# Local attention on one core: whole cells instead of halves, and TensorE's order by kinds of products

## The chip, the core and the metric

The kernel runs on one core of a Trainium2 chip. A core has TensorE (matrix products from SBUF into PSUM; weights are loaded by its own instruction, PEld in the profile), VectorE (DVE), ScalarE (ACT), GpSimd (POOL) and a queue SP that issues DMA transfers. Each engine runs its own instructions in program order and waits for others through semaphores. PSUM has eight banks, and a bank takes 512 float32 values in each of 128 partitions. The metric is the device time of one execution in microseconds; lower is better.

## The reference, cut to what matters

Two transformer layers run over x of shape (4, 512, 128). The first (16 heads of 8, then a mixture of experts) and the attention of the second take the first 0.7 ms and are not touched. The second layer's feed-forward part is itself a stack of six local-attention layers, and this is where the change is:

```python
for i in range(DEPTH):      # 6
    x = attn_layer(shift_tokens(x), Wqkv[i], q_scale[i], k_scale[i], Wo[i]) + x
    x = ffn_layer(shift_tokens(x), ln_g[i], ln_b[i], W1[i], b1[i], W2[i], b2[i]) + x
```

`attn_layer` projects to q, k and v for 16 heads of 64, normalises q and k to length one, multiplies by scales, rotates (xpos), and attends in windows of 32 tokens: each window of 32 queries sees its own window and the one before, so scores are 32 x 64, with a mask, a softmax and a product with 64 rows of v. `ffn_layer` is a layer norm, two products of width 341 with a gelu gate, and a product back. `shift_tokens` moves half of the features by one token.

## The kernel before

**Cells.** The work of the six layers is cut into 96 cells `(l, b, j)`: layer, batch row, and a group of four heads. A loop over n runs a software pipeline: in the turn of cell n, TensorE takes scores and weighing of cell n (or n-1), norms, scaling and values of cells n+1 and n+2, and the projection of cell nx = n+3. All of it is issued inside a manual schedule: the order written in the loop is the order on each engine, and the scheduler only adds the waits.

**Steps of one cell**, with the names of the code:

- `project(n, w)` (line 831): q (w = 0) or k (w = 1) of four heads, 128 x 1024 float32 into `pq`, which fills two banks and has one buffer. `rotate(n, w)` (841 to 844) makes two VectorE products from `pq` and two GpSimd sums. `square(n, w)` (849) is ScalarE's square of `pq` into `sq`, the last reader of `pq`.
- `norms(n)` (859 to 878): sums of squares on TensorE (`nb`, a 128*32 shape), a maximum on VectorE, logarithm and exponential on ScalarE (each with a table load), and four DMAs that spread the result as `rb`. `scale(n)` (886) multiplies k and q by it on GpSimd; `gather(n, w)` (899) rearranges them by four DMAs each into `kd` and `qd`.
- `values(n)` (910 to 920): v into two `pv2` banks, two ScalarE copies to `vo`, three DMAs that make the shifted copy `ve`.
- `scores(n, u)` (933 to 955): for half u of the windows, two mask products (128*128 shape, bfloat16) and 32 small float32 products (64*32 shape, two records each in the profile) into `s2`; then a maximum and a difference on VectorE into `p`. `exponential` (959) is on ScalarE, `normalise` (964 to 966) is a sum, a reciprocal and a product on VectorE.
- `turn(n, u)` (973, 975): four transposes of p on TensorE (128*128) into the one bank of `ps_t`, and a ScalarE copy to `pT`. `weigh(n, u)` (988, 1000): 32 small products with v (64*64 shape) into `ps_o` and `ps_t`, and two ScalarE copies to `oT`.
- `output(n)` (1008, 1009): after every second cell, eight records of the output projection into `py`, and VectorE adds it to the residual `zT`.

**Feed-forward.** After the fourth cell of a batch row a generator `feed(l, b)` is started. It advances where the loop calls `place(name)` with the name it last yielded: Z (issue the shifted load `xsf` from `zT`), B (mean product `lm`, then `l_xc`), D (square), N, L, X (variance product, logarithm, exponential), A (`xn`, two VectorE operations on `l_xc`), then B and D twice (two hidden products `phf` each, and gelu on ScalarE), C (a gate on VectorE), A (two more hidden products and gates), B (`pyf`, three products, and the sum into `zT`). So one batch row's feed-forward is spread over the next batch row's four cells.

**PSUM.** `nb`, `pv2`, `py2`, `lm`, `lv`, `phf` and `pyf` share a pool of two banks (tag `g`), handed out in program order: each new one waits for the readers of the one two places earlier. `pq` has two banks, `s2` two, `ps_t` and `ps_o` one each.

**The loop's order before** for TensorE is: scores half 0, weighing half 1 of the cell before, norms, projection of q, (output), scores half 1, values, transposes half 0, projection of k, weighing half 0, B's products, transposes half 1.

Of the kernel before, what the change touches and what calls it, by code (L numbers as in the profile page):

```python
# [17 lines left out]
F32 = mybir.dt.float32  # L18
BF16 = mybir.dt.bfloat16
AF = mybir.ActivationFunctionType  # L20
ALU = mybir.AluOpType
# [3 lines left out]
B, S, D = 4, 512, 128  # L25
# [21 lines left out]
def adaln_kernel(ctx: ExitStack, tc: tile.TileContext, a: dict):  # L47
# [368 lines left out]
    class First:  # L416
# [41 lines left out]
        def settle(self):  # L458
            pass
# [307 lines left out]
    with ExitStack() as ph:  # L767
# [77 lines left out]

        def square(n, w):
            d = live[n]
            d["sq", w] = work.tile([P, 2, S], F32, name="sq")
            act(d["sq", w], d.pop("pq"), AF.Square)  # L849

        def norms(n):

            d = live[n]
            nb = bank("nb", (P, S // 2))
            for h in range(2):
                for w in range(2):
                    for x in range(2):
                        c = 32 * (2 * w + x)
                        mm(  # L859
                            nb[c : c + 32, :],  # L860
                            nsel,
                            d["sq", w][:, h, x * (S // 2) : (x + 1) * (S // 2)],
                            start=(h == 0),
                            stop=(h == 1),
                            skip_group_check=True,
                        )
            rn = att.tile([P, S // 2], F32, name="rn")
            vec.tensor_scalar(rn, nb, 1e-24, None, ALU.max)
            place("N")
            act(rn, rn, AF.Ln, scale=65536.0)  # L870
            place("L")
            act(rn, rn, AF.Exp, scale=-0.5, bias=nsh_t)
            place("X")
            rb = d["rb"] = work.tile([P, 2, S], F32, name="rb", bufs=1)
            for w in range(2):
                for x in range(2):
                    c = 32 * (2 * w + x)
                    nc.sync.dma_start(
                        rb[:, w, x * (S // 2) : (x + 1) * (S // 2)],
                        rn[c : c + 32, :].unsqueeze(1).broadcast_to([32, 4, S // 2]),  # L880
                    )
# [6 lines left out]
        def gather(n, w):  # L888

            d = live[n]  # L890
            t = d["k" if w else "q"]
            if w:
                d["k"] = kts[n % 2]
                y = d["k"][:, :, WIN:]
            else:
                y = d["q"] = cel.tile([P, 2, S], F32, name="qd", bufs=2)
            for c in range(2):
                for h in range(2):
                    nc.sync.dma_start(y[h::2, c, :], t[64 * c : 64 * c + 64, h, :])  # L899
# [20 lines left out]
            nc.sync.dma_start(ve[64:96, 1:], vo[96:P, 0 : TB - 1])  # L920


        def scores(n, u):
            d = live[n]
            q, k = d["q"], d["k"]


            if u == 0:
                d["s"] = ps_s.tile([P, 2, UW, GK], F32, name="s2")
            s = d["s"][:, :, 4 * u : 4 * u + 4, :]  # L930
            for w in range(2):
                m = wmask_b[:, 1 if u == 0 and w == 1 else 0, 0:4, :]
                mm(s[:, w], ident_b, m, start=True, stop=False, skip_group_check=True)
            for i in range(4):
                for w in range(2):
                    t0 = (u * UW + 2 * i + (w + i + 1) % 2) * WIN
                    for x in range(4):
                        r, c = slice(64 * (x % 2), 64 * (x % 2) + 64), 32 * ((x + w) % 4)
                        mm(  # L939
                            s[c : c + 32, w, i, :],  # L940
                            q[r, x // 2, t0 : t0 + WIN],
                            k[r, x // 2, t0 : t0 + GK],
                            start=False,
                            stop=True,
                            skip_group_check=True,
                        )
            nm = att.tile([P, 2, 4], F32, name="nm2")
            vec.reduce_max(nm, s, axis=AX.X)  # L948
            p = d["p", u] = att.tile([P, UW, GK], F32, name="p2")
            vec.tensor_tensor(  # L950
                p.rearrange("p (i w) k -> p w i k", w=2),
                s,
                nm.unsqueeze(3).broadcast_to([P, 2, 4, GK]),
                ALU.subtract,
            )

        def exponential(n, u):
            p = live[n]["p", u]
            act(p, p, AF.Exp)  # L959

        def normalise(n, u):
            p = live[n]["p", u]
            sm = att.tile([P, UW], F32, name="sm2")
            vec.reduce_sum(sm, p, axis=AX.X)  # L964
            vec.reciprocal(sm, sm)
            vec.tensor_tensor(p, p, sm.unsqueeze(2).broadcast_to([P, UW, GK]), ALU.mult)  # L966

        def turn(n, u):

            p = live[n].pop(("p", u))  # L970
            pt = ps_t.tile([P, 4, P], F32, name="pt2", tag="pt2")
            for i in range(4):
                tr(pt[:, i, :], p[:, 2 * i : 2 * i + 2, :].rearrange("p w k -> p (w k)"), ident)  # L973
            pT = live[n]["pT", u] = att.tile([P, 4, P], F32, name="pT2")
            nc.scalar.copy(pT, pt)  # L975

        def weigh(n, u):
            d = live[n]
            pT = d.pop(("pT", u))

            po = [ps_o.tile([P, 2, 4, WIN], F32, name="po2"), ps_t.tile([P, 2, 4, WIN], F32, name="po2b", tag="pt2")]
            for i in range(4):
                for x in range(4):
                    c = 64 * (x % 2)
                    for w in range(2):
                        r = slice(64 * w, 64 * w + 64)
                        c1 = 32 * ((x + w) % 4)
                        mm(  # L988
                            po[w][c : c + 64, x // 2, i, :],
                            d["v"][(w + i) % 2][r, 2 * u + i // 2, 64 * x : 64 * x + 64],  # L990
                            pT[r, i, c1 : c1 + 32],
                            start=True,
                            stop=True,
                        )
            if u == 0:
                d["o"] = cel.tile([P, 2, 2, S // 2], F32, name="oT2", bufs=2)
            o = d["o"][:, u].rearrange("p h (a w q) -> p (h a) w q", w=4, q=WIN)
            for w in range(2):
                y = po[w].rearrange("p h (a b) q -> p (h a) b q", b=2)
                nc.scalar.copy(o[:, :, 0::3, :] if w else o[:, :, 1:3, :], y)  # L1000

        def output(n):
# [11 lines left out]
        def feed(l, b):  # L1014
# [38 lines left out]
            yield "B"  # L1053
            ge = [one.tile([P, S], F32, name=f"ge{c}") for c in range(3)]
            t0, t1 = hidden(1, 0), hidden(1, 1)
            yield "D"
            gelu(0, t0)
            gelu(1, t1)
            yield "B"
            t0, t1 = hidden(1, 2), hidden(0, 2)  # L1060
            yield "D"
            gelu(2, t0)
            yield "C"
            gate(2, t1)
# [29 lines left out]
        for n in range(-4, NC + 1):  # L1094
            nx = n + 3 if 0 <= n + 3 < NC else None
            here = 0 <= n < NC
            if here:
                scores(n, 0)
            if 0 <= n + 1 < NC:
                scale(n + 1)  # L1100
                gather(n + 1, 1)
            if n > 0:
                weigh(n - 1, 1)
            if here:
                exponential(n, 0)
            if 0 <= n + 2 < NC:
                norms(n + 2)
            elif n + 2 >= NC:
                for name in "NLX":
                    place(name)  # L1110
            place("C")
            if 0 <= n + 1 < NC:
                gather(n + 1, 0)
            if nx is not None:
                l, b, j = cells[nx]
                if l + 1 < DEPTH:
# [3 lines left out]
                        load_rotations(l + 1)  # L1120
                project(nx, 0)
            if here:
                normalise(n, 0)
            if nx is not None:
                rotate(nx, 0)
            if n > 0 and cells[n - 1][2] % 2 == 1:
                output(n - 1)
            place("Z")
            if n + 4 < NC and cells[n + 4][2] == 0:
                b = cells[n + 4][1]  # L1130
                shifted[b] = shift_in(b, xss[b % 2])
            if here:
                scores(n, 1)
            if nx is not None:
                square(nx, 0)
            if 0 <= n + 2 < NC:
                values(n + 2)
            if here:
                exponential(n, 1)
            place("A")  # L1140
            if here:
                turn(n, 0)
                normalise(n, 1)
            if nx is not None:
                project(nx, 1)
                rotate(nx, 1)
            if here:
                weigh(n, 0)
            place("B")
            if here:  # L1150
                turn(n, 1)
            if nx is not None:
                square(nx, 1)
                l, b, j = cells[nx]
                for b1, j1, w, h in turns:
                    if (b1, j1) == (b, j) and l + 1 < DEPTH:
                        rotations(l + 1, w, h)
            place("D")
        while feeds or running:
            for name in "NLXCZABD":  # L1160
                place(name)


# [102 lines left out]
```

## Time and profile before

| | us |
|---|---|
| three runs, median (lowest to highest) | 2494.04 (2487.45 to 2505.30) |
| the profiled execution, its own time | 2490.49 |
| its span, first to last instruction | 2488.7 |
| busy: TensorE / VectorE / ScalarE / GpSimd | 2182.5 / 1524.1 / 1399.9 / 1072.2 |
| mean granted TensorE clock | 0.944 of full speed |

The time of the profiled execution and its span differ by 1.8 us, which lies around the program's own instructions. In the lines of the profile, "L831" is line 831 of the kernel. A row of the order in time gives start, length, engine, line, operation, out<-in, shape and count; matmul lengths are modelled and overlap the next ones, so the price of a block is read from its start to the next block's start. A float32 product of 128x512 shows as two records. Stretches ("2248.59:2265.77") give busy time and count for each engine, then the granted clock, the share of the DMA engines and GB/s. A wait is "who waited <- for whom: total us, times, longest us".

### The profile page before, as it was taken

How to read it: one execution, taken by the hardware profiler on the slowest of the kernel's cores; microseconds unless marked ns; L12 is line 12 of the kernel's file. 1: busy time of each engine (PE TensorE's matmuls, PEld its weight loads, DVE VectorE, ACT ScalarE, POOL GpSimd, SP SyncE). 2: the span in 40 equal slices, each digit the busy share in tenths (PEclk: the TensorE clock that was granted, in tenths of full speed). 3: DMA queues.
4: the chain of work that ended last, by engine and by line, in shares of the span. 5: the costliest groups of instructions: out<-in, count | busy, mean ns of one | idle time of the engine just before them, and what ended most of it. 6: DMA issues, size and time to landing. Idle time of an engine off the chain costs nothing.

```text
span 2488.7 us, 76520 instructions
## 1 busy us (share of the span) xinstructions
PE 2182.5 (88%) x33628; PEld 1246.4 (50%) x33628; DVE 1524.1 (61%) x2258; ACT 1399.9 (56%) x2211; POOL 1072.2 (43%) x690
## 2 busy tenths in 40 slices
PE   6889999886688888999999888999889899889996
PEld 3345454443245555555555555555555555555553
DVE  3454545333266666777677766767667767677763
ACT  1333344534256566766566665667666666676763
POOL 1000101010365565556555565555665556555550
PEclk8999999888789999999999998999999999999998
DMA  2100000000156645566554844557545565555551
GB/s 73 64 2 1 3 1 1 1 1 1 55 133 157 149 114 127 124 174 148 116 131 113 210 111 112 129 124 191 123 117 125 149 170 120 122 119 135 125 137 27
DMA packets 164760, 251.23 MB, mean 101 GB/s; under 512 B 28742, under 2 KB 90380, under 8 KB 163404
## 3 DMA queue, kind: packets, MB, share of 16 engines
q1 hardware_dynamic: 164428, 246.34, 40.9%
q8 instruction: 264, 4.33, 0.7%
q14 instruction: 68, 0.56, 0.1%
HBM read 34.27 MB, written 1.05 MB: 14 GB/s over the span
## 4 chain that ended last, share of the span: by engine, by line
PE 59%; ACT 13%; DVE 9%; issue 7%; SPq 5%; DMA 4%; POOL 3%; ACTq 0%; DVEq 0%; POOLq 0%
PE pq L831 10%; PE phf L1021 5%; PE s L286 5%; PE py L1008 4%; PE po L988 4%; PE nb L859 3%; ACT sq L849 3%; PE s L939 3%; PE pyf L1072 3%; PE ye L360 3%; PE pv L910 2%; DMA xsf<-zT 2%; PE pt L973 2%; DVE qr L841 2%; SPq L899 2%
## 5 line engine op out<-in xcount | busy, mean ns | idle before, releaser
L831 PE MATMUL pq<-xs,wqkv 128*128 128x512 f32 x768 | 393.8, 637 | 21.6 <-ACT sq L849 20.0
L843 POOL TENSOR_TENSOR kr<-kr,ur 128x512 f32<-128x512 f32 x96 | 122.0, 1271 | 499.4 <-DVE ur L842 460.8
L849 ACT ACTIVATE sq<-pq 128x1024 f32<-128x1024 f32 x192 | 197.1, 1027 | 129.9 <-DVE ur L842 126.1
L975 ACT COPY pT<-pt 128x512 f32<-128x512 f32 x192 | 112.5, 586 | 246.4 <-PE pt L973 246.4
L886 POOL TENSOR_TENSOR qr<-qr,rb 128x1024 f32<-128x1024 f32 x96 | 235.4, 2452 | 0.0
L842 DVE TENSOR_TENSOR ur<-pq,tabs 128x1024 f32<-128x1024 f32 x192 | 232.6, 1212 | 0.0
L843 POOL TENSOR_TENSOR qr<-qr,ur 128x512 f32<-128x512 f32 x96 | 123.4, 1286 | 253.3 <-DVE ur L842 252.0
L831 PEld LDWEIGHTS pq<-xs,wqkv 128*128 128x128 f32 x768 | 141.1, 202 | 180.5 <-issue 149.0
L886 POOL TENSOR_TENSOR kr<-kr,rb 128x1024 f32<-128x1024 f32 x96 | 228.6, 2382 | 6.2 <-DMA rb<-rn 6.2
L404 ACT ACTIVATE p<-s 128x1024 f32<-128x1024 f32 (+3 forms) x160 | 104.0, 701 | 188.9 <-PE s L286 150.5
L173 POOL TENSOR_TENSOR ln_rs<-ln_rs,mhalf 128x4 f32<-128x4 f32 x16 | 16.8, 1050 | 443.9 <-DVE ln_rs L172 443.9
L948 DVE TENSOR_REDUCE nm<-s 128x8 f32<-128x512 f32 x192 | 132.1, 688 | 122.0 <-PE s L939 121.9
L964 DVE TENSOR_REDUCE sm<-p 128x8 f32<-128x512 f32 x192 | 130.5, 680 | 112.5 <-ACT p L959 112.3
L910 PE MATMUL pv<-wqkv,xs 128*128 128x256 f32 x768 | 191.5, 392 | 0.8 <-DVE zT L1009 0.8
L1021 PE MATMUL phf<-l_xc,w 128*128 128x512 f32 (+1 forms) x288 | 154.1, 662 | 42.3 <-ACT vo L917 38.3
L939 PE MATMUL s<-kd,qd 64*32 64x64 f32 x12288 | 172.9, 227 | 19.4 <-DMA qd<-qr 17.5
L966 DVE TENSOR_TENSOR p<-p,sm 128x512 f32<-128x512 f32 x192 | 179.6, 936 | 6.6
L1000 ACT COPY oT<-po 128x256 f32<-128x256 f32 x192 | 71.2, 371 | 197.6 <-PE po2b L988 194.5
L1008 PE MATMUL py<-oT,wo 128*128 128x512 f32 x384 | 172.8, 593 | 0.6 <-ACT ge L1026 0.6
L859 PE MATMUL nb<-sq,nsel 128*32 128x256 f32 x1536 | 117.7, 416 | 62.1 <-ACT ge L1026 51.0
L988 PEld LDWEIGHTS po<-pT,vo 64*64 64x64 f32 x3072 | 126.6, 137 | 89.6 <-ACT pT L975 63.0
L988 PE MATMUL po<-pT,vo 64*64 64x32 f32 x3072 | 164.2, 224 | 7.6 <-ACT pT L975 6.8
(198 smaller groups left out, 4987.2 us busy)
## 6 DMA issues: line engine op xcount, KB each, us to landing
rb<-rn SPq DMA_DIRECT2D x384, 128.0 KB
kd<-kr SPq DMA_DIRECT2D x384, 128.0 KB
qd<-qr SPq DMA_DIRECT2D x384, 128.0 KB
ve<-vo SPq DMA_DIRECT2D x96, 256.0 KB
tabs<-in_rope_dram SPq DMA_DIRECT2D x12, 1024.0 KB
ve<-vo SPq DMA_DIRECT2D x96, 128.0 KB
wqkv<-in_Wqkv_dram SPq DMA_DIRECT2D x6, 1536.0 KB
ve<-vo SPq DMA_DIRECT2D x96, 96.0 KB
```

The source lines that it names most:

```text
L831: mm(pq[:, h, :], layers[l][0][:, c0 : c0 + P], shifted[b], start=True, stop=True)
L842: vec.tensor_tensor(u, d["pq"], t[:, 2 * w + 1], ALU.mult)
L843: pool_e.tensor_tensor(r[:, 0, :], r[:, 0, :], u[:, 1, :], ALU.subtract)
L849: act(d["sq", w], d.pop("pq"), AF.Square)
L859: mm(nb[c : c + 32, :], nsel, d["sq", w][:, h, x * (S // 2) : (x + 1) * (S // 2)], start=(h == 0), stop=(h == 1), skip_group_check=True,)
L886: pool_e.tensor_tensor(t, t, d["rb"][:, w, :].unsqueeze(1).broadcast_to([P, 2, S]), ALU.mult)
L910: mm(pv[:, t, :], shifted[b][:, (y + t) * P : (y + t + 1) * P], layers[l][0][:, c0 : c0 + 4 * HDW], start=True, stop=True,)
L939: mm(s[c : c + 32, w, i, :], q[r, x // 2, t0 : t0 + WIN], k[r, x // 2, t0 : t0 + GK], start=False, stop=True, skip_group_check=True,)
L966: vec.tensor_tensor(p, p, sm.unsqueeze(2).broadcast_to([P, UW, GK]), ALU.mult)
L988: mm(po[w][c : c + 64, x // 2, i, :], d["v"][(w + i) % 2][r, 2 * u + i // 2, 64 * x : 64 * x + 64], pT[r, i, c1 : c1 + 32], start=True, st ...
L1008: mm(py, layers[l][1][:, 2 * j - 2 + y, :], o[:, :, y % 2, :], start=(y == 0), stop=(y == 3))
L1021: mm(t[0:m], w1[:, w * DI + r0 : w * DI + r0 + m], xn, start=True, stop=True)
```

## The change

The halves go away. `scores` makes all windows of a cell in one block (two mask products of twice the width, 64 small products); its two VectorE operations become `settle`, for the whole cell (128x1024); `exponential` and `normalise` work on the whole cell; `turn` makes eight transposes into two banks (`ps_o`, `ps_t`) with two copies; `weigh` makes 64 small products into the same two banks, with two copies of 128x512 each in place of four of 128x256. `norms` is split into `norms` and `invert`, which are called one after the other. `sq` gets three buffers for two, `qd` one for two, `p` and `pT` one. In `feed`, gelu waits at a new place G, which the loop calls right behind B.

The loop's order becomes: projection of q, scores (64*32), weighing of the cell before (64*64), norms (128*32), projection of k, output, values, transposes, B's products. Gather of q moves ahead of the norms' DMAs, and loads of a layer's weights and tables to the head of the turn.

```diff
-                y = d["q"] = cel.tile([P, 2, S], F32, name="qd", bufs=2)
+                y = d["q"] = cel.tile([P, 2, S], F32, name="qd", bufs=1)
...
+        def settle(n):
+            d = live[n]
+            s = d.pop("s")
+            nm = att.tile([P, 2, UW], F32, name="nm2")
             vec.reduce_max(nm, s, axis=AX.X)
-            p = d["p", u] = att.tile([P, UW, GK], F32, name="p2")
+            p = d["p"] = att.tile([P, 2 * UW, GK], F32, name="p2", bufs=1)
...
+            for u in range(2):
+                pt = (ps_o, ps_t)[u].tile([P, 4, P], F32, name="pt2", tag="pt2")
+                for i in range(4):
+                    g = 4 * u + i
+                    tr(pt[:, i, :], p[:, 2 * g : 2 * g + 2, :].rearrange("p w k -> p (w k)"), ident)
+                nc.scalar.copy(pT[:, 4 * u : 4 * u + 4], pt)
...
+            po = [(ps_o, ps_t)[w].tile([P, 2, 2, 4, WIN], F32, name=f"po{w}", tag="pt2") for w in range(2)]
```

The loop body of the turn of cell n, after the change, without the conditions on n and nx:

```python
load_layer / load_rotations            # at two cells of a layer
project(nx, 0)
scores(n)
scale(n + 1); gather(n + 1, 1); gather(n + 1, 0)
rotate(nx, 0); square(nx, 0)
settle(n)
weigh(n - 1)
exponential(n)
norms(n + 2); invert(n + 2)            # places N, L, X inside
place("C")
normalise(n)
project(nx, 1); rotate(nx, 1)
output(n - 1)                          # every second cell
place("Z"); shift_in(...)              # at j = 0
values(n + 2)
square(nx, 1)
place("A")
turn(n)
place("B"); place("G")
rotations(l + 1, w, h)                 # at four cells of a layer
place("D")
```

## The prediction

> **What bounds it now.** I read the page first (shares of the engines, chain that ended last), then the busy times of four consecutive cells, the order of TensorE's instructions in one of them, who waited for whom, and the granted clock behind a long wait.
>
> ```profile
> PE 2182.5 (88%) x33628; PEld 1246.4 (50%) x33628; DVE 1524.1 (61%) x2258; ACT 1399.9 (56%) x2211; POOL 1072.2 (43%) x690
> PE 59%; ACT 13%; DVE 9%; issue 7%; SPq 5%; DMA 4%; POOL 3%; ACTq 0%; DVEq 0%; POOLq 0%
> ```
> TensorE is nearly full, and the chain runs mostly through it. The 96 cells stand at 695 to 2438 us, 18.3 us each; only they change. A quiet group (layer 5, batch 1, cells j = 0 to 3):
>
> ```profile
> 2248.59:2265.77 17.18, 16.13 (x312) 9.80 (x310) 13.05 (x18) 10.03 (x16) 8.55 (x6) 1.00 0.59 132
> 2265.77:2281.72 15.95, 14.67 (x309) 9.07 (x307) 14.27 (x18) 11.43 (x19) 9.64 (x6) 1.00 0.61 148
> 2281.72:2300.24 18.52, 16.95 (x314) 10.04 (x312) 12.11 (x17) 13.89 (x20) 9.82 (x7) 1.00 0.47 102
> 2300.24:2320.26 20.02, 16.41 (x313) 9.72 (x311) 13.08 (x19) 13.16 (x19) 11.02 (x8) 1.00 0.49 122
> ```
> Columns: stretch, its length, busy PE, PEld, DVE, ACT, POOL, clock. At full clock four cells take 71.67 us, of which TensorE works 64.16 and waits 7.5. VectorE works 52.5: 73%, a close second, and that matters below.
>
> ```profile
> 2286.52 1.98 PE L831 MATMUL pq<-xs,wqkv 128*128 128x512 f32 x4
> 2288.34 3.60 PE L1008 MATMUL py<-oT,wo 128*128 128x512 f32 x8
> 2291.78 0.38 PE L933 MATMUL s<-wmask_b,ident_b 128*128 128x256 bf16 x2
> 2292.09 0.86 PE L939 MATMUL s<-kd,qd 64*32 64x64 f32 x64
> 2292.88 1.99 PE L910 MATMUL pv<-wqkv,xs 128*128 128x256 f32 x8
> 2294.71 0.60 PE L973 MATMUL pt<-ident,p 128*128 128x128 f32 x4
> 2295.14 1.88 PE L831 MATMUL pq<-xs,wqkv 128*128 128x512 f32 x4
> ```
> Start to start is a block's price: projection 1.82, output 3.44, masks 0.31, half the scores 0.79, values 1.83, half the transposes 0.43; from the same view half the weighing 1.07 and the norm sums 1.00.
>
> ```profile
> ACT sq L849 <- DVE ur L842: 83.6, 86, 3.5
> PE nb L859 <- ACT ge L1026: 51.0, 39, 1.6
> PE phf L1021 <- ACT vo L917: 38.3, 22, 2.9
> PE lm L1036 <- DMA xsf<-zT: 33.7, 22, 3.6
> ```
> These are the waits that interrupt TensorE (total, times, longest). The first says that the square, last reader of the projection's PSUM, starts only after both rotation products of VectorE.
>
> **What is removed.** Starts of single matmuls in the trace give the price of a change of shape: masks follow each other at 109 ns, the first 64*32 score follows the last mask at 203 (94 more); 64*32 to 64*64 and back to 128*128 costs about 134 over the stride, 64*64 to 128*32 133, 128*32 to 128*128 148, 128*128 to 64*64 93. A cell pays eight such changes before and four after; the four that go are 94+134+93+133 = 0.45 us. The first 128*128 product behind a change also takes 1.82 for 1.72; two of these go, 0.2. Together 0.66 us a cell, 63 us in 96 cells.
>
> ScalarE and VectorE save a fixed part per merged instruction. 128x1024 against 128x512 (rotation product 1.21, zT sum 0.68; square 1.03, copy 0.59) puts 512 more elements at 0.53 and 0.44. So maximum and difference cost 1.22 each for 2x0.69, the exponential 1.07 for 2x0.63, the copy of weighed values 0.59 for 2x0.37: 0.9 us a cell of both engines, none of it on TensorE. The norm wait for gelu (51 us) goes: its bank is now asked for 5.7 us into the next cell, behind projection, scores and weighing. Splitting norms moves nothing; three sq and one qd buffers cost nothing while scores (done at 3.7 us) read qd before the next gather. Gather q now stands ahead of rb in SP's queue, both still 8 us early. The loads of weights and tables stand ahead of a cell's gathers: 0 to 15 us over five layers, I take 5.
>
> **What is added.** The halves gave TensorE work while the other half was in softmax. Now one chain runs per cell, and VectorE holds it in program order: rotate(0), settle, normalise, rotate(1), then output's sum or the feed-forward's scaling. I place one cell, from its first projection (0.00 us), at full clock.
> TensorE: projection 1.72, masks 0.53 with the change, scores 1.44 (to 3.69), weighing 2.00 (5.69), norms 1.00 (6.69), projection 1.82 (8.51), [output 3.43], values 1.73, transposes 0.87: 11.11 without output.
> VectorE: rotate 1.81 to 4.16 (starts 1.14 apart), settle to 6.54. ScalarE: two copies from 5.80, exponential 6.78 to 7.84. VectorE: normalise (1.22+0.21+1.22) 7.90 to 10.60, rotate(1) to 12.87. Where gelu ran in the cell before (j = 2, 3), a table load of 1.28 comes before the exponential: rotate(1) ends at 14.15.
>
> - j=0: output ends 11.94, but its zT sum waits for rotate(1): 13.5. The second values product needs py's bank: 0.8 idle. SP is through with rb at 14.05 (3.6 from the exponential's end through both table loads, then 4x0.64); xsf's issue to lm took 2.96 (2261.41 to 2264.37): lm at 17.0, 1.7 idle; it and the next xs: 18.1.
> - j=1: xn follows rotate(1) (0.68+1.38): 14.8. TensorE is through at 11.97: 2.9 idle; two hidden products: 16.65.
> - j=2: zT sum 14.76; the second values product waits for it from 12.8: 2.05 idle; then 0.86, 0.87, 1.72: 18.3.
> - j=3: values copies stand behind exponential and both table loads, at 12.6: hidden products wait from 10.24 to 13.3, 3.06 idle; then 1.72, 0.87, 2.58: 18.45.
>
> Sum 71.5. Check from the other side: work 4x11.11 + 2x3.43 + 11x0.86 = 60.8, idle 0.8+1.7+0.3+2.9+2.05+3.06 = 10.8: 71.6. Against 71.67 the whole saving is eaten: **0 us at full clock**. Queued behind the values product that waits for zT's sum are the transposes, and behind those the feed-forward and the next cell's projection; behind a waiting phf the same, with VectorE's next rotation waiting in turn: nothing on TensorE fills these holes. The pq loop itself (square ends 13.98 to 18) does not bind.
>
> **The clock.** Three waits of 2 to 3 us a group come in place of pieces below 2, and this trace shows what follows:
>
> ```profile
> 935.20:938.40 3.20, 0.03 (x4) 0.01 (x1) 1.90 (x2) 0.65 (x2) 1.22 (x1) 0.94 0.85 199
> 938.40:941.40 3.00, 2.97 (x8) 1.67 (x8) 0.69 (x1) 0.04 (x1) 3.00 (x3) 0.50 0.63 174
> ```
> After 3.2 us without work the clock is 0.50 for 3.4 us. From 694 to 1300 us I count 7 waits over 2 us (8.3 groups), 5 with such a stretch behind them. Three a group instead of 0.8, times 5/7: 1.5 more stretches, each losing 1.7 us of work that the next step waits for: 2.5 us a group, **60 us** in 24 groups. The Trainium skill speaks against the change here: "TensorE: Matmul & The Clock Gate" (Part 1) has the clock halved after an idle window of about 3.4 us; it names the threshold longer than the waits placed here, so by it alone the 60 us would be 0 and the time 2495. The rows show stretches behind shorter waits too (908.3 to 910.6 idle, then 0.50), so I take the count.
>
> **The sum.** 0 + 60 + 5 = +65 us on the profiled execution's 2490.5 (span 2488.7): 2555. That execution lies 3.5 below the median 2494 of the three runs, which differ by 18, so about 1% is what a measurement can tell; I put 2557 against the median.
>
> **Rivals.**
> - Faster: TensorE stays the bound. If VectorE's order costs no more idle than now (7.5 a group), the saved 63 us come through, and no clock is lost: about 2430. For it: PE 88%. Against: VectorE's 12.9 us to the end of rotate(1) in each cell, with nothing for TensorE left behind the transposes. It decides once idle falls below 9 a group.
> - No change: full-clock balance, stretches at half clock no more frequent than now, because waits of 2 to 3 us straddle a window: 2495, 2470 to 2518.
> - Much slower: the normalising product meets GpSimd on every cell. Its mean is 0.93 against 0.69 alone, 1.51 in one cell here; doubled, it would cost up to 1.2 us more a cell on that VectorE chain, 29 us, and with all four waits a group halving the clock (3.4 stretches more, 24x3.4x1.7 = 139): 2490+29+139 = 2660. For it: GpSimd's scaling lies right ahead; against: it should be through at 7 us.
> - The change does not do what it says: the extra 94 to 148 ns are weight loads rather than the change of shape, and stay. Then 63 us come on top of the forecast: 2620. Against: the excess stands at every change of shape and nowhere else within a block.
>
> **How the numbers follow.** Forecast 0.45; much slower 0.10 and price stays 0.08, both slower; no change 0.17; faster 0.20. The forecast's own range is 2520 to 2600; the range 2455 to 2645 leaves out the outer part of the faster case and of the slower ones. Slower by over 1%: 0.63, within 1%: 0.17, faster: 0.20.
>
> **What would show it.** PE busy time should fall by some 60 us at equal clock. Right: waits phf <- vo of 3 us each, phf <- xn of l_xc near 3 us, values <- zT of 2 us; norms <- gelu gone; more half-clock stretches; j = 1 longer than 15.95, j = 3 shorter than 20.02. Wrong, if idle a group stays near 7.5, if rotate(1) ends before 12 us of a cell, or if the projection waits for the square.

## The result: 9% slower, and the profile after

The changed kernel takes 2715.23 us (median of four runs, 2709.68 to 2723.55) against 2490.74 for the kernel before in the same comparison: a ratio of 1.0896, 95% interval 1.0849 to 1.0943, or +224 us. Forecast was 2557, with a range of 2455 to 2645. The direction was right, the size was not. The profiled execution took 2716.49 us (span 2714.3); its page has these lines, engines' busy time and the chain that ended last:

```profile
PE 2244.5 (83%) x33340; PEld 1273.2 (47%) x33436; DVE 1414.8 (52%) x1778; ACT 1374.5 (51%) x1923; POOL 1064.9 (39%) x690
PE 59%; issue 13%; ACT 12%; DVE 6%; DMA 5%; SPq 3%; POOL 1%; ACTq 0%; DVEq 0%; POOLq 0%
```

TensorE is less full (83% for 88%), and on the chain "issue", time in which an engine waits for nothing that the profile shows, has gone from 7% to 13%. The same group of four cells as in the prediction (layer 5, batch 1; columns as there, the clock is the third number from the end):

```profile
2448.12:2469.24 21.12, 17.91 (x307) 10.47 (x308) 11.38 (x13) 10.24 (x14) 11.09 (x7) 0.92 0.56 130
2469.24:2491.59 22.35, 17.50 (x303) 10.21 (x304) 12.17 (x13) 13.14 (x18) 10.83 (x7) 0.85 0.45 101
2491.59:2512.30 20.71, 18.38 (x310) 10.45 (x310) 10.70 (x12) 12.81 (x16) 8.24 (x6) 0.92 0.39 90
2512.30:2532.80 20.50, 17.79 (x307) 10.68 (x308) 13.94 (x15) 11.24 (x15) 10.52 (x7) 0.92 0.45 103
```

Four cells take 84.68 us for 71.67, every cell is longer than 20 us, and no cell keeps the full clock. TensorE's waits in the stage of the cells (total, times, longest):

```profile
PE po L995 <- issue: 152.8, 79, 5.1
PE phf L1027 <- ACT vo L921: 43.4, 21, 2.9
PE phf L1027 <- ACT pT L982: 33.7, 17, 2.2
PE pv L914 <- ACT vo L921: 31.1, 46, 0.7
PE nb L859 <- issue: 21.6, 13, 4.6
PE phf L1027 <- DVE l_xc L1058: 15.3, 6, 2.9
```

The norms' wait for gelu is gone, as forecast. The largest wait is new, and no step of the forecast has it: the weighing (`po`) stands still 79 times in the 96 cells, 1.9 us each, and for nothing that another engine does. The order in time shows where, on TensorE (start, length, engine, line, what, count, idle before):

```profile
1989.87 0.38 PE L934 MATMUL s<-wmask_b,ident_b 128*128 128x512 bf16 x1
1990.18 1.55 PE L940 MATMUL s<-kd,qd 64*32 64x64 f32 x128
1991.66 0.24 PE L995 MATMUL po<-pT,vo 64*64 64x32 f32 x1
...
1994.67 0.24 PE L995 MATMUL po<-pT,ve 64*64 64x32 f32 x1 [1.60 <-issue]
1995.49 1.49 PE L859 MATMUL nb<-sq,nsel 128*32 128x256 f32 x16
```

Scores take 1.48 us, start to start, and the weighing begins at once. Then it pauses for 1.60 us until 1994.67, and ends at 1995.49: 3.83 us for a block that takes 2.00 where nothing pauses it. What that does to ScalarE (the first row is VectorE's), and to the clock (four stretches, then one that ends where the half clock begins):

```profile
1993.38 1.22 DVE L955 TENSOR_TENSOR p<-s,nm 128x1024 f32<-128x1024 f32 x1
1995.60 1.07 ACT L1006 COPY oT<-po 128x512 f32<-128x512 f32 x2 [2.27 <-PE po L995]
1996.69 1.28 ACT L964 ACT_TABLE_LOAD   x1
1997.99 1.06 ACT L964 ACTIVATE p<-p 128x1024 f32<-128x1024 f32 x1
```
```profile
1989.50:1994.60 5.10, 3.52 (x211) 2.78 (x210) 4.71 (x4) 1.02 (x1) 4.56 (x3) 1.00 0.56 118
1994.60:1996.00 1.40, 1.33 (x59) 1.12 (x63) 0.00 (x1) 0.40 (x1) 0.19 (x1) 1.00 0.99 205
1996.00:1999.40 3.40, 3.40 (x15) 1.28 (x8) 0.75 (x2) 3.35 (x5) 0.00 (x0) 0.50 0.28 57
1999.40:2003.00 3.60, 3.60 (x10) 1.55 (x9) 3.53 (x5) 3.16 (x4) 0.00 (x0) 1.00 0.00 0
```
```profile
1992.59:1996.00 3.41, 1.81 (x92) 1.49 (x88) 1.98 (x2) 1.14 (x2) 2.20 (x2) 1.00 0.69 143
```

The copies `oT`, which read the weighing's result, stand ahead of the exponential on ScalarE, which waits 2.27 us for them. The softmax's difference on VectorE was ready at 1994.60 (1993.38 + 1.22), but the exponential starts at 1997.99. And 1.3 us after the pause the clock is 0.50 for 3.4 us. A pause of 1.6 us was enough here: in the 3.41 us before, TensorE was busy for 1.81. "TensorE: Matmul & The Clock Gate" (Part 1) of the Trainium skill names an idle window of about 3.4 us; these rows show less, and they decide. Over the whole trace (from 694 us on) the clock changes only on a grid with steps of 3.41 us. It went from full to half 87 times, each time behind a step in which TensorE was busy for at most 63%; in the 398 steps behind which it stayed full, TensorE was busy for at least 43%. So a short pause can be enough where it leaves its step half empty. Of the 79 pauses, 44 have a stretch at half clock that begins within 3.5 us of their end.

**Where the time went**, as a mean over a group of four cells, from one group's first masks to the next group's. Work is TensorE's busy time with half of what it did at half clock taken off.

| us a group | before | after | difference |
|---|---|---|---|
| work, at full clock | 63.87 | 62.32 | -1.55 |
| idle, put down to "issue" | 0.72 | 7.53 | +6.81 |
| other idle | 6.79 | 6.66 | -0.13 |
| lost at half clock | 2.38 | 6.86 | +4.48 |
| sum | 73.77 | 83.37 | +9.60 |

24 groups times 9.60 is 230 us, the whole difference. So two terms have to be explained: pauses that no engine causes, and the clock.

**What the pauses are.** The page's list of queues has an instruction queue: in the kernel before 264 transfers and 4.33 MB, after it

```profile
q8 instruction: 263, 4.31, 0.7%
```

That is 16,384 bytes each. TensorE's records, 33340 + 33436, divided by 263 are 254: so a transfer brings some 256 instructions, and the queue looks like TensorE's supply. The transfers' own times say so too: each of the 79 pauses at `po` ends 0.8 to 1.6 us (median 1.4) after the end of such a transfer. A small float32 product has two matmul records and two weight loads: four instructions. 64 scores and 64 products with values are 512 instructions that want 1.48 + 2.00 = 3.5 us. All other blocks are slow in instructions: the projection's 8 take 1.7 us. My theory: TensorE draws the weighing faster than its instructions come. Rivals: the merged block is held up by what its products read or write (PSUM banks, v, memory traffic), and the pauses only mark it; or pauses cost little and the whole-cell VectorE chain costs it all, as forecast.

### The profile page after: what moved, and what is told of

The parts are those of the page before. It is cut to its first block, busy times and chain, and to the rows that moved or that the text cites. A ratio compares the mean times of both kernels' runs of the same rounds, so it can differ in the third digit from the quotient of the medians.

```text
span 2714.3 us, 75685 instructions
## 1 busy us (share of the span) xinstructions
PE 2244.5 (83%) x33340; PEld 1273.2 (47%) x33436; DVE 1414.8 (52%) x1778; ACT 1374.5 (51%) x1923; POOL 1064.9 (39%) x690
## 4 chain that ended last, share of the span: by engine, by line
PE 59%; issue 13%; ACT 12%; DVE 6%; DMA 5%; SPq 3%; POOL 1%; ACTq 0%; DVEq 0%; POOLq 0%
PE pq L831 10%; PE po L995 7%; PE phf L1027 6%; PE s L940 5%; PE py L1014 4%; PE s L286 4%; PE nb L859 3%; PE pyf L1078 2%; PE ye L360 2%; ACT L874 2%; PE pv L914 2%; PE p L342 2%; ACT p L964 2%; PE pt L981 2%; PE s L282 1%
## 5 line engine op out<-in xcount | busy, mean ns | idle before, releaser
L995 PE MATMUL po<-pT,vo 64*64 64x32 f32 x6144 | 235.6, 228 | 96.0 <-issue 96.0
L841 DVE TENSOR_TENSOR qr<-pq,tabs 128x1024 f32<-128x1024 f32 x96 | 117.6, 1225 | 315.0 <-PE pq L831 300.0
L995 PE MATMUL po<-pT,ve 64*64 64x32 f32 x6144 | 231.2, 228 | 56.8 <-issue 56.8
L995 PEld LDWEIGHTS po<-pT,vo 64*64 64x64 f32 x6144 | 215.8, 143 | 104.4 <-issue 95.8
L995 PEld LDWEIGHTS po<-pT,ve 64*64 64x64 f32 x6144 | 211.5, 143 | 66.4 <-issue 66.2
L1006 ACT COPY oT<-po 128x512 f32<-128x512 f32 x192 | 103.3, 589 | 244.6 <-PE po L995 244.5
L914 PEld LDWEIGHTS pv<-wqkv,xs 128*128 128x128 f32 x768 | 143.0, 191 | 111.3 <-ACT vo L921 49.5
L921 ACT COPY vo<-pv 128x512 f32<-128x512 f32 x192 | 107.7, 582 | 167.4 <-PE pv L914 167.2
L868 DVE TENSOR_SCALAR rn<-nb 128x256 f32<-128x256 f32 x96 | 40.8, 425 | 279.8 <-PE nb L859 265.0
L859 PE MATMUL nb<-sq,nsel 128*32 128x256 f32 x1536 | 154.8, 521 | 21.6 <-issue 21.6
```

The costliest lines, as they stand in the source:

```text
L841: vec.tensor_tensor(r, d["pq"], t[:, 2 * w], ALU.mult)
L859: mm(nb[c : c + 32, :], nsel, d["sq", w][:, h, x * (S // 2) : (x + 1) * (S // 2)], start=(h == 0), stop=(h == 1), skip_group_check=True,)
L914: mm(pv[:, t, :], shifted[b][:, (y + t) * P : (y + t + 1) * P], layers[l][0][:, c0 : c0 + 4 * HDW], start=True, stop=True,)
L995: mm(po[w][c : c + 64, i // 4, x // 2, i % 4, :], d["v"][(w + i) % 2][r, i // 2, 64 * x : 64 * x + 64], pT[r, i, c1 : c1 + 32], start=True ...
```

## Experiments: is it the supply of instructions?

**The same work, put in two places.** In the kernel before, one half's weighing is issued twice, the same 128 instructions more a cell. In one run it is the half that stands right behind scores; in the other, the half that stands behind a projection.

```diff
-            for i in range(4):
+            for i in [*range(4)] * (2 if u == 1 else 1):     # behind scores
+            for i in [*range(4)] * (2 if u == 0 else 1):     # behind the projection
```

> Edit of the kernel before: the second half's weighing products (which follow the scores directly) are issued twice, with the same result; 128 instructions and 0.93 us more a cell, 89 us in all. Supply theory: the run behind the masks grows from 256 to 384 instructions without a pause, TensorE waits 0.5 to 1.5 us at 'issue' in most cells: 50 to 140 us of 'issue' idle and a time of 2610 to 2720. VectorE theory: only the work counts, partly hidden: 2530 to 2580, 'issue' idle below 25 us, and the same as the next kernel within 1%.

> Edit of the kernel before: the first half's weighing products (which follow a projection of 1.8 us with 8 instructions) are issued twice, with the same result; also 128 instructions and 0.93 us more a cell, but in a run of 256 that stands by itself. Supply theory: 'issue' idle stays below 30 us, time 2540 to 2590. VectorE theory: the same time as the kernel with the doubled second half, 2530 to 2580.

Measured: behind scores 2633.35 us, 1.0545 (1.0488 to 1.0601); behind the projection 2575.65, 1.032 (1.0255 to 1.0385). TensorE's waits at `po` and `po2b` put down to "issue", first behind scores, then behind the projection:

```profile
PE po L988 <- issue: 50.6, 27, 5.0
PE po2b L988 <- issue: 47.4, 29, 5.6
```
```profile
PE po2b L988 <- issue: 6.9, 7, 1.5
PE po L988 <- issue: 6.0, 5, 1.5
```

The same number of products of the same shape on the same banks costs 58 us more behind scores, and pauses of 98 us stand there for 13. What differs is the place, and with it how many instructions are drawn in a row. The count of transfers settles whose instructions they are: 128 more in each of 96 cells make 312 transfers for 264 in both runs, 48 more, 256 instructions each.

**Nothing but TensorE.** A kernel of its own, which computes nothing of the reference and was timed in one execution: eight rounds of 64 score products in a run, the same beside 64 transfers, then single rounds with large products between them.

> Not the model: TensorE alone. After a warm-up of large products come 8 rounds of the 64 small score products (4 instructions each, 2048 in a run without a wait), the same again beside 64 transfers of 128 KB, and then 12 single rounds with 3.4 us of large products between them. Supply theory: a round in the long run takes 3.4 to 4.2 us, with pauses of about 2 us that nothing explains, 27 to 34 us for eight; beside the transfers longer still; a single round takes 1.4 to 1.6 us without a pause. If instructions are not what limits: eight rounds in 11.3 to 12.5 us, single rounds the same.

TensorE's order in time, groups of records with the idle time before them:

```profile
21.14 2.09 PE L42 MATMUL s<-x 64*32 64x64 f32 x191
25.26 1.83 PE L42 MATMUL s<-x 64*32 64x64 f32 x128 [2.03 <-issue]
28.99 2.04 PE L42 MATMUL s<-x 64*32 64x64 f32 x128 [1.89 <-issue]
32.72 2.04 PE L42 MATMUL s<-x 64*32 64x64 f32 x128 [1.69 <-issue]
...
109.36 1.48 PE L42 MATMUL s<-x 64*32 64x64 f32 x128
110.78 1.55 PE L32 MATMUL w<-x 128*128 128x512 f32 x3
```

No other engine works in the first run, and the pauses are there: after each 128 matmul records (with their 128 weight loads 256 instructions) 1.4 to 2.0 us, and a new lot every 3.5 to 3.7 us. Eight rounds take 27.3 us (to 48.47), where one by itself takes 1.42: 2.4 times as long. Beside the transfers they take 28.8, 5% more, so traffic adds little and is not needed. The clock falls here too; the page's line of granted clock, in 40 slices, has it at half in both long runs:

```profile
PEclk9999995555557999965555599999999999999999
```

So the pause is a limit of supply, some 256 instructions each 3.5 to 3.7 us, and needs no neighbour. The transfers' times show the cycle: one starts 1.0 to 1.8 us after the lot before it comes into use, lasts 0.9 to 1.7 us, and all 14 pauses end 1.2 to 1.5 us after a transfer's end. No transfer in these runs starts before the last one has been put to use; why not was not found.

## Experiments: what does the pause cost the kernel?

**Norms between.** In the changed kernel the norm sums (1.0 us, 32 instructions) go between scores and weighing.

```diff
                 settle(n)
+            if 0 <= n + 2 < NC:
+                norms(n + 2)
             if n > 0:
                 weigh(n - 1)
...
-                norms(n + 2)
```

> Edit of the kernel after: the norm sums (32 instructions that take 1.0 us) stand between scores and weighing instead of behind weighing; as many changes of TensorE's shape, same work. Supply theory (TensorE runs out of instructions, which come in transfers of 16 KB, when 512 instructions of small products stand in one run): the pause of 1 us lets a transfer in, TensorE's idle time before weighing put down to 'issue' (152.8 us) falls to 40 to 100 us, and the time from 2715 to 2600 to 2660. VectorE theory (the loss is VectorE's order, as predicted: 7 us of other waits a group): 'issue' idle and time stay, 2700 to 2730. Clock theory (small products by themselves make the clock drop): time 2700 to 2730, some 84 stretches at half clock as in the kernel after.

Measured 2744.53, 1.0992 (1.0931 to 1.1052): not faster, a miss. The pauses did fall by nearly half:

```profile
PE po L995 <- issue: 82.4, 76, 4.2
PE phf L1027 <- ACT vo L921: 84.8, 22, 3.9
```

But the weighing ends at 7.8 to 9.5 us of a cell (medians by j), no earlier than before the edit: 1.0 us of norms stand where 1.0 us of pause stood. The `oT` copies and the exponential come no earlier, and idle time only changes its name: a group has 3.5 us of "issue" for 7.5, and 12.9 of other waits for 6.7. So shorter pauses alone pay nothing while the exponential stands behind the weighing; whether that is the reason, the next edits test.

**Values between.** The values products (1.7 us) go there instead.

```diff
                 settle(n)
+            place("C")
+            if 0 <= n + 2 < NC:
+                values(n + 2)
             if n > 0:
                 weigh(n - 1)
...
```

> Edit of the kernel after: the values products (16 instructions, 1.73 us) stand between scores and weighing; two more changes of shape a cell, some 0.35 us or 34 us in all, and the exponential comes 1.7 us later. Supply theory: 'issue' idle falls from 177 us (po and nb) to under 40, stretches at half clock from 84 to under 60, time 2530 to 2620. VectorE theory: 2720 to 2800, since the chain through VectorE begins later and nothing else is gained. Clock theory: the stretches stay above 75 and the time above 2680.

Measured 3412.47, 1.3696 (1.3607 to 1.3784): inconclusive, by a fault of the edit. v has three buffers, and values of cell n+2 write the one that the weighing of n-1 then reads, so the weighing uses a later cell's v and must wait for its shifted copy:

```profile
PE po L995 <- DMA ve<-vo: 484.0, 93, 8.6
```

Pauses fall to 3.7 us, but nothing can be read from the time.

**Exponential first**, alone and with norms between. On ScalarE the exponential now stands ahead of the `oT` copies; the weighing itself stays where it is.

```diff
-            if n > 0:
-                weigh(n - 1)
             if here:
                 exponential(n)
+            if n > 0:
+                weigh(n - 1)
```

> Edit of the kernel after: the exponential stands ahead of weighing in the program, so ScalarE no longer takes the two copies of weighed values (which wait for the end of weighing) before it. TensorE's order is unchanged. Theory of both together (missing instructions delay the end of weighing by 2 us, and the copies carry that into the exponential and so into VectorE's whole chain): the pauses stay, 130 to 190 us of 'issue' idle, but the exponential starts 6.7 us into a cell (8.0 with a table load) for 8.8 to 10.5, the second rotation ends at 13 to 14.5 for 15 to 17, and the time falls to 2540 to 2630. If the pauses cost only their own time on TensorE: 2690 to 2720.

> Both edits on the kernel after: exponential ahead of weighing, and the norm sums between scores and weighing. Theory of both together: 'issue' idle 70 to 95 us as with the norm sums alone, the exponential at 6.7 us, time 2520 to 2600, at least 10 us under the exponential alone. If the exponential's place does not matter: 2730 to 2750 as with the norm sums alone.

Measured: 2645.39, 1.0642 (1.0576 to 1.0709), 15 us past its range; with norms between 2576.81, 1.033 (1.0274 to 1.0385), inside its range. ScalarE in a cell of the first:

```profile
2006.83 1.06 ACT L964 ACTIVATE p<-p 128x1024 f32<-128x1024 f32 x1 [1.31 <-DVE p L955]
2007.89 1.07 ACT L1006 COPY oT<-po 128x512 f32<-128x512 f32 x2
```

The exponential waits for VectorE now, not for the weighing, and starts at 6.7 us of a cell (median, for each j) where it started at 8.7 to 10.8. One swap on ScalarE gives back 70 us, with pauses nearly unchanged (7.53 to 6.95 us a group). With the chain freed, norms between do pay: 69 us more, where alone they paid nothing. Of 224 us, 138 went with the two edits, which are aimed at what stands behind the pause and at its length (the second also brings the norms forward, which was not tried apart). Not all of the pause is gone; what is left in that kernel:

```profile
PE po L995 <- issue: 91.2, 76, 5.5
PE lm L1042 <- DMA xsf<-zT: 58.3, 23, 3.8
PE phf L1027 <- DVE l_xc L1058: 52.7, 18, 4.0
PE phf L1027 <- ACT vo L921: 32.5, 21, 1.8
```

Two of these are waits that the forecast placed: `phf` for `l_xc` at its price, 2.9 us each, and `lm`, 2.5 us for 1.7.

**Weighing late.** To take the pauses away altogether, the weighing goes behind the second projection, with values and output after it, and the exponential stays ahead.

```diff
...
                 rotate(nx, 1)
+            if n > 0:
+                weigh(n - 1)
+            if 0 <= n + 2 < NC:
+                values(n + 2)
             if n > 0 and cells[n - 1][2] % 2 == 1:
                 output(n - 1)
```

> Edit of the kernel after: exponential ahead of weighing, and weighing moved behind norm sums and the second projection (2.8 us and 48 instructions between scores and weighing), then values, then output. One more pair of shapes, 0.23 us or 22 us in all. Supply theory: 'issue' idle below 30 us, 64 or fewer stretches at half clock, time 2500 to 2580. If small products by themselves stop TensorE wherever they stand: 'issue' idle above 120 us.

Measured 2592.84, 1.0412 (1.0373 to 1.0451), 13 us over its range.

```profile
PE lm L1042 <- DMA xsf<-zT: 71.1, 24, 3.7
PE pq L831 <- ACT sq L849: 51.8, 73, 2.3
PE po L995 <- issue: 12.8, 9, 2.3
PE py L1014 <- ACT vo L921: 56.8, 40, 1.5
```

The pauses are gone (0.52 us a group, as before the change) and the weighing takes its 2.0 us. Other idle time is 11.5 a group, near the forecast's 10.8, though it is not the forecast's order: weighing, values and output stand later, and the projection now waits for the square, which the forecast had ruled out for its own. rotate(1) ends at 12.82 us (median) for j = 0, 2 and 3, where the hand placement had 12.87 or 14.15. For j = 1 it ends at 14.26: in 21 of 24 groups that cell begins at half clock, behind the wait of `lm`. This order of whole cells is 4% slower than halves with hardly a pause left in it.

**The clock.** In the kernel with exponential first and norms between, six constant products (some 1.3 us) fill TensorE ahead of `lm` and of the first hidden product, so that these waits are shorter for the clock; their results are overwritten.

```diff
+            def fill(t):
+                for _ in range(6):
+                    mm(t[:, 0:P], mean_w, mean_w, start=True, stop=True)
...
             pm = bank("lm")
+            fill(pm)
             mm(pm, mean_w, xsf, start=True, stop=True)
...
```

> On the edit of the kernel after with the exponential ahead and the norm sums between (2577 us, 35 stretches at half clock): six products of constants (1.3 us, 24 instructions) are put ahead of the feed-forward's mean product and of its first hidden product, where TensorE waits 2.5 and 2.9 us; their result is overwritten. Clock theory (waits of 2 to 3 us halve the clock and the next products pay): under 25 stretches, 2540 to 2568. If the clock's stretches cost nothing because VectorE is late anyway: 2570 to 2595.

Measured 2554.34, 1.0257 (1.0209 to 1.0305), 22 us below the kernel it starts from; the two intervals overlap a little. In the profiles the stretches at half clock fall from 35 to 20 and a group from 77.56 to 76.78, although TensorE does 3.1 us more work in it. What is lost at half clock falls from 2.52 to 1.70 us a group. That agrees with a clock term that is real, at some 0.8 us a group for these two waits.

## Experiments: can the halves be kept and something gained?

Three versions of the kernel before. The first asks for gelu at a place G ahead of `square`, to take the norms' wait away. The second keeps halves, but transposes the first half ahead of the second half's scores and weighs it right behind them: six changes of shape a cell for eight. The third has both.

```diff
+            place("G")                       # gelu_early: gelu waits here, ahead of square(nx, 1)
...
             if here:                         # halves_by_kind
+                turn(n, 0)
                 scores(n, 1)
...
                 exponential(n, 1)
+                weigh(n, 0)
```

> One part of the change alone, on the kernel before: gelu at the place G, which here stands right behind the second half's transposes and ahead of the square. The wait of the norm sums for gelu (51.0 us in 39 cells) should shrink to under 20 us. Theory of both together: 2455 to 2490, since TensorE then goes on to the projection 1 us earlier in two cells of four. If the cells are bound by VectorE behind it: 2485 to 2500.

> On the kernel before, halves kept: transposes of the first half go ahead of the second half's scores, and the first half's weighing right behind those scores, so that each run of small products has 256 instructions and is followed by at least 4 us of large products. Six changes of shape a cell for eight, 0.33 us or 32 us of TensorE less. Supply theory: 'issue' idle stays below 35 us, time 2450 to 2490. If every pair of small blocks in a row stalls: 'issue' idle above 100 us and 2560 or more.

> Both of these edits on the kernel before: 2420 to 2475 if their gains add; the better of the two alone if the waits they remove stand behind the same chain.

Measured: 2502.91, 1.0037 (1.0007 to 1.0068); 2531.92, 1.0159 (1.0127 to 1.0192); 2546.14, 1.022 (1.0181 to 1.0258). All three miss, none beats the kernel before. New waits, from the first and from the second:

```profile
PE nb L859 <- ACT sq L849: 24.7, 41, 3.0
PE nb L859 <- ACT ge L1026: 17.9, 32, 0.6
```
```profile
PE pt L973 <- DVE p L966: 45.2, 30, 4.9
```

33 us less behind gelu are 25 us more behind the square that gelu now precedes. Fewer changes of shape bring the transposes ahead of the softmax they need: 45.2 us of waits, against 1.0 in the kernel before and 32 that the changes were to save. The theory of supply was right in the second run (some 30 us of "issue", expected below 35), but not about the time. In these halves, then, the order with eight changes of shape hides the softmax better than the one with six.

## Why the prediction missed by 160 us, step by step

In the forecast's own terms, for a group of four cells: idle time 10.8 forecast and 14.2 measured, work 60.8 and 62.3, loss by the clock 2.5 and 4.5 more than before. The three differences, 6.9 us times 24, are 165 us; the profiled execution lies 161.5 above the forecast's 2555.

- **Changes of shape: right in sign, too large.** 0.66 us a cell was forecast, 0.39 came (1.55 a group, 37 us in all). The blocks by themselves have their forecast prices where nothing disturbs them: weighing 2.00, norms 1.00, values 1.73, transposes 0.87. Where the other 0.27 went was not resolved. The sum of blocks, 60.8 us of work, was also 0.7 below what the forecast's own figures give (64.16 less four savings of 0.66). The rival that the excess stays with weight loads does not fit: scores fall from 2 x 0.79 to 1.48, weighing from 2 x 1.07 to 2.00.
- **The placing of a cell: VectorE right, the weighing wrong.** Settle ended at 6.66 to 6.74 us (forecast 6.54). The weighing was placed to end at 5.69 and ended at 7.7 to 8.4 (medians by j). This is the step that failed: its price, 2.00 us, was twice the 1.07 of a half that stood behind a projection or behind half the scores, and I took it to hold for 256 instructions right behind 256 others. From there the placing itself predicts the damage: copies, exponential (8.7 to 10.8 for 6.78 or 8.06), rotate(1) at 15.0 to 17.0 for 12.87 or 14.15. What the runs showed in its place is a limit of supply, 256 instructions each 3.5 to 3.7 us, and so a pause of 1.9 us in 79 of 96 cells. "0 us at full clock" rested on that price first, but not on it alone: weighing late, with hardly a pause, still takes 74.7 us a group at full clock against 71.4 before.
- **Idle time.** Forecast 10.8 a group, measured 14.18, of which 7.53 are pauses. The pauses took the place of waits that I had named: values never waited for `zT` (its waits are for `vo`, 0.7 each), `phf` for `vo` was 2.1 each for 3, and for `l_xc` 2.6 each but only 6 times. With the pauses gone (weighing late) the other waits are 11.5.
- **The clock.** Forecast 1.5 more stretches a group, 60 us; measured 29 stretches before and 84 after, 2.3 a group more, and 4.48 x 24 = 107 us. The sort of term was right, its size was not. The pauses come on top, one in four of five cells, 44 of 79 with a stretch at half clock behind them. Without them the term was too large: weighing late has 46 stretches and loses 24 us more than before, for 60.
- **The loads** (+5 us): no run shows this term by itself. `pq` waits for `xs` 7.0 us in 7 waits, which is too small to tell.
- **By cells.** j = 1 became longer, as forecast: a mean of 20.4 for 15.4. j = 3 should have been shorter than 20.02 and was 21.1 (20.8 before). PE busy did not fall but rose by 62 us, since the page counts busy time at whatever clock; at equal clock it fell by 37.
- **Rivals.** "Faster" fell with its own condition, idle below 9 a group. "Much slower" named a product on VectorE that meets GpSimd; it was not that: this product took 1.22 to 1.23 us in each of the 96 cells. That the kernel with the exponential first and norms between ends at +82 us, near the forecast's +63, is no support for the forecast: its clock term is nearly absent there (2.52 us a group for 2.38 before), and pauses are still in it.

What is left in the two best orders of whole cells, by the sums of the table above, times 24: with norms between, pauses +77 us, other waits +40, clock +3, work -29; with weighing late, pauses -5, other waits +114, clock +24, work -29. This divides the time and does not show which wait would go by itself.

A hint stood in the views of before, unread: TensorE's 67,256 records in 264 transfers of instructions, and among its waits a few behind the small products that no engine causes, of up to 2.1 us:

```profile
q8 instruction: 264, 4.33, 0.7%
PE po L988 <- issue: 6.3, 5, 2.1
```

What stays open is the cause of the remaining 82 to 98 us of the whole-cell orders. Waits and clock are both in the profile, but of these only the clock was varied by itself, once, with overlapping intervals.

## What to carry to other kernels

Count instructions, not only time: here TensorE gets 256 instructions each 3.5 to 3.7 us once what lies ready is used up. Runs of 512 instructions wanted in 3.5 us paused in 79 of 96 cells, 258 to 510 instructions behind the first mask, however ready their data were; so put large products between two such blocks. A block of many small products should not stand, through its readers on another engine, ahead of the operation that starts the longest chain; one swap on ScalarE was worth 70 us. And merging halves saves fixed costs that are easy to count (1.2 to 1.6 us of work a group here), while the waits that it leaves uncovered have to be found by placing a whole cell, with every block's price taken where the block will stand.

## What the runs showed of the hardware

- TensorE's instructions arrive in transfers of 16 KB, 256 instructions (12,288 more of them make 48 more transfers). In a run of small products a new lot can be used every 3.5 to 3.7 us, also with nothing else running: pauses of 1.4 to 2.0 us, 27.3 us for what takes 8 x 1.42 by itself. Each pause ends some 1.4 us after the end of a transfer.
- Such a run brings the granted clock to half (0.59 on average over the 27.3 us alone), though no pause in it is longer than 2.03 us and TensorE is busy for 15.2 of 27.3 us.
- The clock changes on a grid of 3.41 us. In the changed kernel it fell to half only behind steps in which TensorE was busy for 63% or less; above that it stayed full, and between 43% and 63% both occurred.
- In the changed kernel successive cells keep a beat: stretches at half clock began at 1996.0, 2016.5, 2037.0, 2057.4, 2077.9 and 2098.4 us, 20.5 us or six steps of the grid apart. Whether the clock holds the cells to it or the cells the clock was not tried.
